# First layer of a two-layer selective-scan network: the sum over states kept in PSUM, powers taken downwards, carries of two states gathered on 128 rows

## The chip, the cores and the metric

The kernel runs on one core of a Trainium2 chip. The metric is the device time of the whole program in microseconds (us), the median of three runs. All arithmetic is fp32. The engines are PE (TensorE), DVE (VectorE), ACT (ScalarE), POOL (GpSimd) and SP (the queue that issues DMAs); each takes its own instructions in program order.

## The reference

The input is x, 4 images of 64x64 positions with 192 channels. Two layers follow, each a projection to 384 inner channels, four selective scans over the positions (rows, columns and both backwards), a norm, a gate and a projection back. The change touches the scans of the first layer alone. For each image, each of its four directions k and each inner channel d they are

```
delta = softplus(dts + bias)                      # per position l and channel d
h_n(l) = exp(-n * delta(l)) * h_n(l-1) + delta(l) * u(l) * B_n(l)     n = 1..16
y(l)   = sum over n of C_n(l) * h_n(l)  (+ u(l) * D)
```

because the logs of A are those of 1 to 16, so that state n decays with n times the same exponent (the kernel tests this, and falls back on another path where it does not hold).

## The kernel before

**Tiling.** The 4096 positions of a direction are cut into rounds of `RW` = 31 (`NR` = 133 rounds). A tile has 128 rows, two halves of 64. A half has two directions with 31 positions each, and 2 more rows, the last ones, in which a state enters from the round before and leaves for the next. The free dimension `W` = 1536 is four images of 384 channels. With cum, the sum of delta inside the round, each state is a matrix product: x_n = delta*u*exp(n*(cum-shift)) is multiplied by a masked triangle that carries B_n, and the product by C_n*exp(-n*(cum-shift)).

**A step** is one state of one round, so there are 16 steps in a round. Each step s has these parts:

- `grown` (L1005) makes x of step s+6 from x of the step before by one more factor g: 512 columns on DVE (its factor g0 lies in PSUM), 1024 on POOL. For the first state it starts from `dtu`.
- `decay` (L990, ACT) makes es = exp(-n*cum) over all 1536 columns, and `b_mask` (L996, ACT) four masked triangles `b`, two steps ahead.
- `mix` (L1011, PE) multiplies b by x into a bank q. It is called four times in a step, with two 64x64 matmuls each.
- `weigh` (L1021, DVE) makes t = q * C_n * es, four times in a step, from PSUM into SBUF.
- `add_y` (L1030, PE) sums t over the states, two steps later, by matmuls with the identity into four banks yp: again eight matmuls in a step.
- `carry_out` and `carry_in` (L985, L981, SP) take the last two rows of each half of t to DRAM, and bring them 16 steps later into the same two rows of x.

**A round's preparation** lies between the steps of the rounds before it. `Round.steps` gives it offsets, and `planned` places it. `v` (PE) and `parts` (ACT) make the argument of softplus; `exp`, `log` (ACT), `plus`, `rest`, `total` (POOL) take it apart; `delta` (PE) sums two terms of it by identity matmuls with the halves turned over; `keep_dt` (ACT) and then `times_u` (DVE, L878) read the result; `sums` (PE) and `grow` (ACT) make g; `sums_d` (PE) and `keep_sums` (ACT) make cum; `keep_total` stores its last rows to DRAM for a test of the range after the scans (`reach`, L668 and L670). `load_xd`, `load_u`, `load_bc`, `load_y` and `store_y` are DMAs on SP. `end_y` (DVE, L927) adds yp to the y of earlier rounds.

**What sets the order.** All five queues are written out by hand in one loop over s (`manual_schedule`): program order is the order of emission. The PSUM banks are four for yp, one for g0 and three, one pool, for q and for the bank `m` of the preparation. In one pass of the loop ACT gets decay and the masks of s+2 and then its planned work; DVE gets the four `weigh` of s, with planned work after the second, and then `grown`; PE gets the `mix` of s+1 and the `add_y` of s-2 in turn, with planned work after the second pair and at the end.

Of the kernel before, what the change touches and what calls it, by code (L numbers as in the profile page):

```python
# [15 lines left out]
L = HW * HW  # L16
# [13 lines left out]
RW = 31  # L30
# [542 lines left out]
class FirstLayer(Stage):  # L573
# [3 lines left out]
    def __init__(self, tc, ctx, consts, w, dram, good):  # L577
# [4 lines left out]
        self.uT, self.bc, self.xd, self.y_row, self.y_col, self.tot, self.carry, self.zeros = dram  # L582
# [10 lines left out]
        self.mask = load("mask", [128, HALF])  # L593
# [6 lines left out]
        self.shift = wp.tile([128, 1], F32, name="shift_f")  # L600
        nc.vector.memset(self.shift, -SHIFT)
# [5 lines left out]
        with tc.tile_pool(name="d4", bufs=1) as pd:  # L607
# [24 lines left out]
            nc.sync.dma_start(self.y_col[L // 2 - 2 : L // 2 + 2], z[:4].rearrange("p (b e) -> p b e", b=NB))  # L632
            for n in range(NS):
                nc.sync.dma_start(self.carry[n].rearrange("c q r f -> (c q) (r f)"), z[:KD])
# [28 lines left out]
    def reach(self):  # L663
        nc = self.tc.nc
        with self.tc.tile_pool(name="reach", bufs=1) as pool:
            n = NR * KD * W // 128
            t = pool.tile([128, n], F32, name="tot")
            nc.sync.dma_start(t, self.tot.rearrange("(p f) -> p f", p=128))  # L668
            top = pool.tile([128, 1], F32, name="tot_top")
            nc.vector.tensor_reduce(top, t, mybir.AxisListType.X, ALU.max)  # L670
            nc.vector.tensor_scalar(top, top, REACH / NS - SHIFT, None, ALU.is_le)
            nc.vector.tensor_tensor(self.good, self.good, top, ALU.min)
# [71 lines left out]
    def scans(self):  # L744
        nc, tc = self.tc.nc, self.tc
        with ExitStack() as ctx:
            pool = lambda name, bufs, **k: ctx.enter_context(tc.tile_pool(name=name, bufs=bufs, **k))
            p1, p2 = pool("b1", 1), pool("b2", 2)
            p_x, p_e, p_t, p_b = pool("bx", 7), pool("be", 4), pool("bt", 4), pool("bb", 3)
            ps_y = pool("psy", 1, space=bass.MemoryType.PSUM)  # L750
            ps_q = pool("psq", 3, space=bass.MemoryType.PSUM)
            ps_g = pool("psg", 1, space=bass.MemoryType.PSUM)
            ident, mask, tri = self.ident, self.mask, self.tri
            N = NR * NS
            sets = lambda t: t.rearrange("p (b e) -> p b e", b=NB)
# [3 lines left out]
            top = lambda k: k // 2 * HALF + k % 2 * RW  # L759

# [7 lines left out]
            c_in = [p1.tile([128, NB, NS], F32, name=f"c_in{i}") for i in range(2)]  # L768
            for b, c in zip(b_in, c_in):
                nc.sync.dma_start(b, self.w["b_last"])  # L770
                nc.vector.memset(c, 1.0)
# [6 lines left out]
            def runs(k, r, most, turned=False):  # L778

                row, lo, n = block(k, r)  # L780
                while n:
                    m = min(n, most, HW - lo % HW) if turned else min(n, most)
                    yield row, lo, m
                    row, lo, n = row + m, lo + m, n - m
# [6 lines left out]
            class Round:  # L791

                def __init__(self, r):
                    self.r = r
                    self.b, self.c = b_in[r % 2], c_in[r % 2]
# [9 lines left out]
                def load_u(self):  # L805
                    for k in range(KD):
                        for row, lo, n in runs(k, self.r, 16, k % 2 == 1):
# [3 lines left out]
                def load_bc(self):  # L811
                    for k in range(KD):
                        at = k * 2 * NS
                        for row, lo, n in runs(k, self.r, RW, k % 2 == 1):
# [3 lines left out]
                            for c in range(2):  # L818
                                to = c * HALF + k % 2 * RW + row
                                of = bc_dram[:, 2 * c : 2 * c + 2, at + NS : at + 2 * NS]  # L820
                                nc.sync.dma_start(
                                    self.c[to : to + n, k // 2 * 2 : k // 2 * 2 + 2], place(of, k, lo, n)
                                )

                def bank(self):
                    self.m = ps_q.tile([128, LC], F32, name="m", tag="q")
# [38 lines left out]
                def rest(self):  # L865
                    nc.gpsimd.tensor_tensor(self.d, self.e, self.d, ALU.subtract)  # L866

                def total(self):
                    nc.gpsimd.tensor_tensor(self.l, self.l, self.d, ALU.add)  # L869

                def delta(self, i):
                    one = lambda a, b: ident[half(a), half(a)]
                    self.swap(i, [(one, lambda a, b, t=t: t[half(a), cols(b)]) for t in (self.l, self.up)])
# [11 lines left out]
                def sums(self, i):  # L885
                    self.bank()
                    nc.tensor.matmul(self.m, tri, self.dt[:, wide(i)], start=True, stop=True)  # L887

                def grow(self, i):
                    if i == 0:  # L890
                        self.g0 = ps_g.tile([128, LC], F32, name="g0")
                        to = self.g0
                    else:
                        if i == 1:
                            self.g = p2.tile([128, W - LC], F32, name="g")
                        to = self.g[:, wide(i - 1)]
                    nc.scalar.activation(to, self.m, AF.Exp, bias=shift)  # L897
# [4 lines left out]
                def keep_sums(self, i):  # L902
                    if i == 0:
                        self.cum = p2.tile([128, W], F32, name="cum")
                    nc.scalar.activation(self.cum[:, cols(i)], self.m[:, :DI], AF.Identity, bias=shift)

                def keep_total(self):
                    to = tot[self.r * KD * W : (self.r + 1) * KD * W]
                    for c in range(2):
                        nc.sync.dma_start(to.rearrange("(c q f) -> c q f", c=2, q=2)[c], end(self.cum, c))  # L910

                def load_y(self):
                    r = self.r
                    if r == MIDDLE:
                        for k in (2, 3):
                            nc.sync.dma_start(yold[top(k) : top(k) + RW], zeros)
                    for k in range(KD):
                        if (k % 2 == 1 and r < MIDDLE) or (k > 1 and r == MIDDLE):
                            continue
                        for row, lo, n in runs(k, r, 16):  # L920
                            row += top(k)
                            nc.sync.dma_start(sets(yold)[row : row + n], (y_row, y_col)[k % 2][lo : lo + n])

                def end_y(self, b):
                    if b == 2:
                        self.y = p1.tile([128, W], F32, name="yt")
                    nc.vector.tensor_add(self.y[:, cols(b)], self.yp[b][:, :DI], yold[:, cols(b)])  # L927

                def store_y(self):
                    for k in range(KD):  # L930
                        for row, lo, n in runs(k, self.r, 16):
                            row += top(k)
                            to, of = (y_row, y_col)[k % 2][lo : lo + n], sets(self.y)[row : row + n]
# [5 lines left out]
                def steps(self):  # L939

                    s = lambda f, *a: (lambda: f(*a))
                    r = [(-32, "sp", self.load_xd), (-20, "sp", self.load_u), (-8, "sp", self.load_bc)]
                    for i in range(NB):
                        r += [(i - 24, "pe", s(self.v, i)), (i - 23, "act", s(self.parts, i))]
                        r += [(i - 14, "pe", s(self.delta, i)), (i - 13, "dve", s(self.times_u, i))]
                        r += [(i - 13, "act", s(self.keep_dt, i))]
                        r += [(i - 8, "pe", s(self.sums_d, i)), (i - 7, "act", s(self.keep_sums, i))]
                    r += [(-19, "act", self.exp), (-18, "act", self.log), (-18, "pool", self.plus)]
                    r += [(-17, "pool", self.rest), (-16, "pool", self.total)]
                    r += [(-10, "pe", s(self.sums, 1)), (-9, "act", s(self.grow, 1))]  # L950
                    r += [(-9, "pe", s(self.sums, 2)), (-8, "act", s(self.grow, 2))]
                    r += [(-7, "pe0", s(self.sums, 0)), (-7, "late", s(self.grow, 0))]
                    r += [(-3, "sp", self.keep_total), (6, "sp", self.load_y), (NS + LAG + 1, "sp", self.store_y)]
                    for i, b in enumerate((2, 0, 3, 1)):
                        r += [(NS + LAG, f"dve{i}", s(self.end_y, b))]
                    return r

            w_dt, one, shift, zeros, tot = self.w_dt, self.one, self.shift, self.zeros, self.tot
            uT, bc_dram, xd_dram, y_row, y_col, carry = self.uT, self.bc, self.xd, self.y_row, self.y_col, self.carry
            MIDDLE = L // 2 // RW  # L960
            LAG = 2
# [12 lines left out]
            xs, es, bs, qs, ts = {}, {}, {}, {}, {}  # L974
            of = lambda s: (rounds[s // NS], s % NS)
            end = lambda t, c: t[c * HALF + 2 * RW : (c + 1) * HALF]

            def carry_in(s):
                for r in range(2):
                    to = end(xs[s], r).rearrange("q (c f) -> q c f", c=2)  # L980
                    nc.sync.dma_start(to, carry[s % NS][:, :, r, :].rearrange("c q f -> q c f"))  # L981

            def carry_out(s):
                for c in range(2):
                    nc.sync.dma_start(carry[s % NS][c].rearrange("q r f -> q (r f)"), end(ts[s], c))  # L985

            def decay(s):
                it, n = of(s)
                es[s] = p_e.tile([128, W], F32, name="es")
                nc.scalar.activation(es[s], it.cum, AF.Exp, scale=-(n + 1.0))  # L990

            def b_mask(s, i):
                it, n = of(s)
                if s not in bs:
                    bs[s] = p_b.tile([128, NB, HALF], F32, name="b")
                nc.scalar.mul(bs[s][:, i, :], mask, it.b[:, i, n : n + 1])  # L996

            def grown(s, engine):
                it, n = of(s)
                if s not in xs:  # L1000
                    xs[s] = p_x.tile([128, W], F32, name="x")
                part = slice(0, LC) if engine is nc.vector else slice(LC, W)
                x = it.dtu if n == 0 else xs[s - 1]
                g = it.g0 if engine is nc.vector else it.g
                engine.tensor_tensor(xs[s][:, part], x[:, part], g, ALU.mult)  # L1005

            def mix(s, r, j):
# [775 lines left out]
```

## Time and profile before

| what | us |
|---|---|
| median of three runs | 11298.84 (11295.07 to 11307.86) |
| profiled execution | 11290.43, span 11288.6 |
| first `weigh` to last `weigh` | 712.8 to 9533.7 |
| PE, DVE, ACT, POOL busy, share of the span | 87%, 70%, 71%, 60% |
| the same in one round, 5000 to 5066.5 | 60.0, 49.4, 49.9, 47.6 of 66.5 |

The scans of the first layer take 8821 of the 11289 us; the projection before them takes some 0.7 ms and what follows them 1.75 ms. A group line reads: line, engine, operation, output<-inputs, shape, count | busy time, mean ns of one | idle time of the engine ahead of it, and who ended most of it. A timeline line reads: start, length, engine, line, operation, count, and the idle time ahead of it with its releaser. PE shows each fp32 matmul as two instructions, so a `mix` call has four.

### The profile page before, as it was taken

What the parts mean: (1) busy time and instruction counts of PE and PEld (TensorE: products, weight loads), DVE (VectorE), ACT (ScalarE), POOL (GpSimd) and SP (SyncE); (2) the same over time, 40 slices, a digit from 0 to 9 for tenths busy, and PEclk for the clock granted to TensorE, in tenths of its full rate; (3) what the DMA queues carried; (4) which work ended last, traced back from release to release, by engine and by line L of the source; (5) the groups of instructions that cost most, each with busy time, mean ns of one, the idle gap of its engine ahead of it and who ended that gap; (6) DMA issues with size and microseconds to landing.
All of it is one profiled execution on the core that took longest, in us unless ns stands there. A gap on an engine that the chain in (4) does not pass through costs nothing. (4 is left out here: it accounts for less than half of the span.)

```text
span 11288.6 us, 244138 instructions
## 1 busy us (share of the span) xinstructions
PE 9828.6 (87%) x85544; PEld 4313.8 (38%) x85544; DVE 7946.4 (70%) x13822; ACT 7976.7 (71%) x15454; POOL 6738.5 (60%) x2912
## 2 busy tenths in 40 slices
PE   8989899989998999898989998899889997488677
PEld 4533333333333333333333333333333333454366
DVE  2347777777777777777777777777777777478675
ACT  3357777777777777777777777777777776566587
POOL 0047777777777777777777777777777775300270
PEclk9999999999999999999999999999999999788688
DMA  4421111111111111112222222222222223943358
GB/s 148 165 83 42 45 43 45 42 45 43 45 42 45 43 45 42 45 43 47 50 49 51 48 50 49 51 48 50 49 51 48 50 48 87 265 137 120 143 143 276
DMA packets 667786, 836.25 MB, mean 74 GB/s; under 512 B 305814, under 2 KB 558243, under 8 KB 665822
## 3 DMA queue, kind: packets, MB, share of 16 engines
q1 hardware_dynamic: 661566, 813.80, 27.3%
q0 software_dynamic: 4992, 6.68, 0.4%
q8 instruction: 698, 11.44, 0.4%
q14 instruction: 530, 4.34, 0.1%
HBM read 468.75 MB, written 351.35 MB: 73 GB/s over the span
## 5 line engine op out<-in xcount | busy, mean ns | idle before, releaser
L1011 PE MATMUL q<-x,b 64*64 64x384 f32 x34048 | 6151.7, 492 | 858.4 <-DVE dtu L878 618.9
L1005 POOL TENSOR_TENSOR x<-x,g 128x1024 f32<-128x1024 f32 x1995 | 4730.0, 2371 | 2299.3 <-PE q L1011 1668.3
L1030 PE MATMUL yp<-t,ident 64*64 64x384 f32 x34048 | 6097.5, 494 | 0.0
L1021 DVE SCALAR_TENSOR_TENSOR t<-q,c_in,es 128x384 f32<-128x384 f32 x8512 | 4945.1, 614 | 1082.5 <-PE q L1011 505.9
L1011 PEld LDWEIGHTS q<-x,b 64*64 64x64 f32 x34048 | 2172.8, 132 | 3836.0 <-DVE t L1021 1451.1
L990 ACT ACTIVATE es<-cum 128x1536 f32<-128x1536 f32 x2128 | 3152.5, 1481 | 0.9 <-DVE t L1021 0.9
L1030 PEld LDWEIGHTS yp<-t,ident 64*64 64x64 f32 x34048 | 2069.6, 132 | 757.4 <-issue 660.6
L996 ACT ACTIVATE b<-mask_f,b_in 128x64 f32<-128x64 f32 x8512 | 2255.6, 341 | 3.5 <-PE yp L1030 3.1
L1005 DVE TENSOR_TENSOR x<-x,g 128x512 f32<-128x512 f32 x1995 | 1353.9, 679 | 0.2
L883 ACT COPY dt<-m 128x384 f32<-128x384 f32 x532 | 255.2, 480 | 1359.8 <-PE m L833 1359.8
L878 DVE TENSOR_TENSOR dtu<-m,ut 128x384 f32<-128x384 f32 x532 | 296.8, 558 | 1221.8 <-ACT dt L883 1221.8
L460 PE MATMUL pp<-xT,w_in 96*128 96x512 f32 x1536 | 710.4, 614 | 20.5 <-ACT pad L1230 20.0
L897 ACT ACTIVATE g<-m,shift_f 128x512 f32<-128x512 f32 x399 | 271.2, 680 | 634.2 <-PE m L887 634.1
L862 POOL TENSOR_SCALAR d<-e 128x1536 f32<-128x1536 f32 x133 | 196.5, 1477 | 676.6 <-ACT e L854 676.6
L1244 DVE SCALAR_TENSOR_TENSOR acc<-pad,conv_w_s,acc 128x2048 f32<-128x2048 f32 x192 | 440.7, 2345 | 47.8 <-ACT acc L1242 46.5
L833 PE MATMUL m<-w_dtk_f,xd 26*64 26x384 f32 x2128 | 460.0, 511 | 8.9 <-DMA xd<-xd 8.9
L866 POOL TENSOR_TENSOR d<-e,d 128x1536 f32<-128x1536 f32 x133 | 464.2, 3490 | 0.1
L869 POOL TENSOR_TENSOR l<-l,d 128x1536 f32<-128x1536 f32 x133 | 463.1, 3482 | 0.1
L887 PE MATMUL m<-dt,steps_f 128*128 128x512 f32 x798 | 450.1, 646 | 0.0
L833 PE MATMUL m<-l,ident 64*64 64x384 f32 x2128 | 433.9, 486 | 15.5 <-POOL l L869 15.5
L833 PE MATMUL m<-up,ident 64*64 64x384 f32 x2128 | 433.6, 486 | 0.0
L1005 POOL TENSOR_TENSOR x<-dtu,g 128x1024 f32<-128x1024 f32 x133 | 313.8, 2359 | 200.2 <-PE q L1011 163.4
(201 smaller groups left out, 8258.1 us busy)
## 6 DMA issues: line engine op xcount, KB each, us to landing
x<-carry SPq DMA_DIRECT2D x4256, 12.0 KB
carry<-t SPq DMA_DIRECT2D x4256, 12.0 KB
ut<-uT SPq DMA_DIRECT2D x528, 96.0 KB
zg<-gate SPq DMA_DIRECT2D x64, 768.0 KB
ut<-uT SPq DMA_DIRECT2D x414, 90.0 KB
yold<-y_row SPq DMA_DIRECT2D x263, 96.0 KB
y_row<-yt SPq DMA_DIRECT2D x263, 96.0 KB
y_col<-yt SPq DMA_DIRECT2D x263, 96.0 KB
```

What stands on the lines that cost most here:

```text
L460: self.tc.nc.tensor.matmul(pp, self.w_in[:, i, e * 128 : (e + 1) * 128], self.xT[:, i, t * LC : (t + 1) * LC], start=(i == 0), stop=(i == ...
L833: nc.tensor.matmul(self.m[half(b), :DI], w(a, 2 * b + j), t(a, 2 * b + j), start=n == 0, stop=n == len(terms) - 1, skip_group_check=True,)
L866: nc.gpsimd.tensor_tensor(self.d, self.e, self.d, ALU.subtract)
L869: nc.gpsimd.tensor_tensor(self.l, self.l, self.d, ALU.add)
L887: nc.tensor.matmul(self.m, tri, self.dt[:, wide(i)], start=True, stop=True)
L990: nc.scalar.activation(es[s], it.cum, AF.Exp, scale=-(n + 1.0))
L996: nc.scalar.mul(bs[s][:, i, :], mask, it.b[:, i, n : n + 1])
L1005: engine.tensor_tensor(xs[s][:, part], x[:, part], g, ALU.mult)
L1011: nc.tensor.matmul(q[half(c), :DI], bs[s][half(r), b, :], xs[s][half(r), cols(b)], start=True, stop=True, skip_group_check=True,)
L1021: nc.vector.scalar_tensor_tensor(ts[s][:, cols(i)], qs.pop((s, r, j))[:, :DI], it.c[:, i, n : n + 1], es[s][:, cols(i)], ALU.mult, ALU.mult)
L1030: nc.tensor.matmul(it.yp[2 * c + j][half(r), :DI], ident[half(c), half(c)], ts[s][half(c), cols(2 * r + j)], start=n == 0, stop=n == NS - ...
L1244: nc.vector.scalar_tensor_tensor(acc, part(tap), weight(tap), acc, ALU.mult, ALU.add)
```

## The change

The sum over n is evaluated as a polynomial from the highest power down. Four accumulators `accs` stay in PSUM for the whole stage. In each step `mix` adds the product of state n onto them, and `weigh` multiplies them in place by the ratio C_n/C_(n-1) and by fd = exp(shift-cum), so that the next, lower state is added to it. The states thus go from 16 to 1 (`state(s)` = 16 - s%16): x starts at exp(16*(cum-shift)) and is multiplied by f = exp(shift-cum) from step to step.

- Removed: `decay` over 1536 columns, `add_y`, the tile t, `rest` and `total` on POOL, and the DRAM copy of the totals with its reading back in `reach`.
- Rows: `RW` is 30 and NR 137. Each half now has four rows at its end: the carry of an even state goes through one pair, that of an odd state through the other. `masks` has a form for each, `hold` holds a finished even carry while the odd state is added.
- Carries: at every second step (odd state) `keep_end` copies all four accumulators to SBUF on ACT, ahead of `weigh`; `shrink` (two DMAs) spreads the four last rows of each half over 64 rows of 96; `decay` (ACT, now 128x96), `settle` (POOL) and one `carry_out` DMA follow.
- Preparation: `delta` has four terms in place of two (it does the work of `rest` and `total`); `fall` makes f and `first` the first power g, both on ACT from the same bank; `keep_sums` writes fd as well as cum; `invert` (DVE) and `ratios` (POOL) make the ratios. The first x of a round is made by POOL alone, in three pieces. `m` has three banks of its own.
- End of a round: `add_old` adds the old y by a matmul onto each accumulator, `end_y` copies it out on ACT; both stand in the loop ahead of the `mix` that starts the accumulator anew.
- `load_y`, `store_y`, `load_u` cut their DMAs elsewhere; `test` (DVE) keeps a running maximum of the totals.

```diff
-RW = 31
+RW = 30
...
-                def rest(self):
-                    nc.gpsimd.tensor_tensor(self.d, self.e, self.d, ALU.subtract)
-                def total(self):
-                    nc.gpsimd.tensor_tensor(self.l, self.l, self.d, ALU.add)
                 def delta(self, i):
-                    one = lambda a, b: ident[half(a), half(a)]
-                    self.swap(i, [(one, lambda a, b, t=t: t[half(a), cols(b)]) for t in (self.l, self.up)])
+                    terms = [(ident, self.e), (minus, self.d), (ident, self.l), (ident, self.up)]
...
+                def add_old(self, i):
+                    for c in c_tiles:
+                        nc.tensor.matmul(
+                            accs[i][half(c), :DI], ident[half(c), half(c)], yold[half(c), cols(i)],
+                            start=False, stop=True, skip_group_check=True,
+                        )
...
-                    nc.vector.tensor_add(self.y[:, cols(b)], self.yp[b][:, :DI], yold[:, cols(b)])
+                    nc.scalar.copy(self.y[:, cols(i)], accs[i][:, :DI])
...
+                        r += [(i - 16, "pe", s(self.delta, i)), (i - 15, "dve", s(self.times_u, i))]
+                        r += [(i - 15, "act", s(self.keep_dt, i))]
+                        r += [(i - 9, "pe", s(self.sums_d, i)), (i - 8, "act", s(self.keep_sums, i))]
                     r += [(-19, "act", self.exp), (-18, "act", self.log), (-18, "pool", self.plus)]
+                    for i in (1, 2):
+                        r += [(i - 12, "pe0", s(self.sums, i)), (i - 11, "act", s(self.fall, i)), (i - 11, "act", s(self.first, i))]
+                    r += [(-7, "pe0", s(self.sums, 0)), (-6, "act", s(self.first, 0)), (-6, "act", s(self.fall, 0))]
...
+            def keep_end(s, i):
+                if i == 0:
+                    sxs[s] = p2.tile([128, W], F32, name="sx")
+                nc.scalar.copy(sxs[s][:, cols(i)], accs[i][:, :DI])
...
+                        accs[i][half(c), :DI], bs[s][half(r), b, :], xs[s][half(r), cols(b)],
+                        start=s % NS == 0, stop=state(s) == 1, skip_group_check=True,
...
+                part = accs[i][:, :DI]
                 nc.vector.scalar_tensor_tensor(
-                    ts[s][:, cols(i)], qs.pop((s, r, j))[:, :DI], it.c[:, i, n : n + 1], es[s][:, cols(i)], ALU.mult, ALU.mult
+                    part, part, it.ratio[:, i, n - 1 : n], it.fd[:, cols(i)], ALU.mult, ALU.mult
                 )
...
+                    if pair(s - 1):
+                        shrink(s - 1)
+                    if pair(s - 5):
+                        carry_out(s - 5)
                     if on(s + AHEAD - 2):
                         carry_in(s + AHEAD - 2)
                     planned(s, "sp")
+                    if pair(s):
+                        for i in order:
+                            keep_end(s, i)
+                    if pair(s - 2):
+                        decay(s - 2)
                     if on(s + 2):
-                        decay(s + 2)
                         for i in range(NB):
                             b_mask(s + 2, i)
                     planned(s, "act")
...
+                    for at, i in enumerate(order):
                         if on(s):
+                            weigh(s, i)
+                        if at == 1:
                             planned(s, "dve")
                     if on(s + AHEAD):
                         grown(s + AHEAD, nc.vector)
+                    for at, i in enumerate(order):
+                        if on(s) and state(s) == 1:
+                            of(s).add_old(i)
+                            of(s).end_y(i)
                         if on(s + 1):
+                            mix(s + 1, i)
+                        if at == 1:
                             planned(s, "pe0")
                     planned(s, "pe")
```

## The prediction

> **What bounds the kernel now.** I read the page first, its busy times and groups:
>
> ```profile
> PE 9828.6 (87%) x85544; PEld 4313.8 (38%) x85544; DVE 7946.4 (70%) x13822; ACT 7976.7 (71%) x15454; POOL 6738.5 (60%) x2912
> ...
> L1030 PE MATMUL yp<-t,ident 64*64 64x384 f32 x34048 | 6097.5, 494 | 0.0
> L1021 DVE SCALAR_TENSOR_TENSOR t<-q,c_in,es 128x384 f32<-128x384 f32 x8512 | 4945.1, 614 | 1082.5 <-PE q L1011 505.9
> ...
> L990 ACT ACTIVATE es<-cum 128x1536 f32<-128x1536 f32 x2128 | 3152.5, 1481 | 0.9 <-DVE t L1021 0.9
> ```
>
> PE looks full, but the change takes half of its matmuls away, so its share says little about the time after. Then DVE's timeline over one round, for the steps one by one:
>
> ```profile
> 5036.41 2.20 DVE L1021 SCALAR_TENSOR_TENSOR t<-q,c_in,es 128x384 f32<-128x384 f32 x4
> 5038.52 0.68 DVE L1005 TENSOR_TENSOR x<-x,g 128x512 f32<-128x512 f32 x1
> 5039.11 2.20 DVE L1021 SCALAR_TENSOR_TENSOR t<-q,c_in,es 128x384 f32<-128x384 f32 x4
> ...
> 5046.37 1.14 DVE L1021 SCALAR_TENSOR_TENSOR t<-q,c_in,es 128x384 f32<-128x384 f32 x2
> 5049.77 0.56 DVE L878 TENSOR_TENSOR dtu<-m,ut 128x384 f32<-128x384 f32 x1 [2.25 <-ACT dt L883]
> 5050.24 1.13 DVE L1021 SCALAR_TENSOR_TENSOR t<-q,c_in,es 128x384 f32<-128x384 f32 x2
> 5051.30 0.68 DVE L1005 TENSOR_TENSOR x<-x,g 128x512 f32<-128x512 f32 x1
> 5051.89 1.14 DVE L1021 SCALAR_TENSOR_TENSOR t<-q,c_in,es 128x384 f32<-128x384 f32 x2
> ```
>
> The reader is to see two kinds of step. A bare one takes 5039.11-5036.41 = 2.70 us: DVE without a gap. One with `times_u` takes 5051.89-5046.37 = 5.52. The other steps with planned work took 3.0 to 6.2. A round took 66.5 us, of which DVE worked 49.4 and ACT 49.9: **no engine is full; in-order queues waiting for one another set the time.** So the question is what the new queues wait for. PE's timeline ahead of that `times_u`, then ACT's:
>
> ```profile
> 5047.04 0.54 PE L1011 MATMUL q<-x,b 64*64 64x384 f32 x2 [0.71 <-DVE t L1021]
> 5047.06 0.54 PE L1030 MATMUL yp<-t,ident 64*64 64x384 f32 x2
> 5047.42 0.49 PE L1011 MATMUL q<-x,b 64*64 64x384 f32 x2
> 5047.43 0.49 PE L1030 MATMUL yp<-t,ident 64*64 64x384 f32 x2
> 5047.75 0.81 PE L833 MATMUL m<-l,ident 64*64 64x384 f32 x4
> 5048.40 0.81 PE L833 MATMUL m<-up,ident 64*64 64x384 f32 x4
> ```
>
> ```profile
> 5022.93 0.49 ACT L850 ACTIVATE e<-m 128x384 f32<-128x384 f32 x1 [0.21 <-PE m L833]
> 5023.31 0.49 ACT L851 ACTIVATE up<-m 128x384 f32<-128x384 f32 x1
> ...
> 5049.26 0.48 ACT L883 COPY dt<-m 128x384 f32<-128x384 f32 x1 [2.11 <-PE m L833]
> ```
>
> The prices, all from this round: a `weigh` lasts 0.61, the next starts 0.53 later, `grown` on DVE takes 0.59 of the queue; from the start of a `weigh` to the matmul that waits for it 0.67; a pair of matmuls 0.87 (5047.04 to 5047.91), its row half free again after 0.71; each identity term of `delta` 0.65, two terms 1.46; PE's end to ACT or DVE 0.05 to 0.08. A small ACT copy lasts 0.48 and takes 0.38 of the queue (5022.93 to 5023.31), with a bias 0.58 and 0.49, at 512 columns with a bias 0.59; four masks take 0.95; `exp` and `log` 1.37 and 1.47.
>
> [...] `times_u` and `keep_dt` only read m, and DVE waits 2.25 us for ACT. [...] No row here has DVE writing PSUM[...]. ACT's g took 0.66 into PSUM (5015.05) and 0.69 into SBUF (5004.64), so I take 0.53. [...] after 2.71 us of idle at 725.8, two terms of `delta` took 2.8, at a clock of 0.51.
>
> **The change part by part, by queue and round** (16 steps).
>
> PE loses 128 of its `mix`/`add_y` matmuls in 256, and gains 16 for `delta` and 8 for `add_old`. It was not waited for by its amount, so this is worth nothing by itself: `add_y` had no idle time of its own. But each accumulator is now a chain: `weigh`, `mix`, (`keep_end`,) `weigh`. From one `weigh` to the next on the same bank that is 0.67+0.87+0.07 = 1.6, with the copy 2.1; DVE comes back after 2.71. So a bare step stays at 2.71.
>
> DVE: 64 `weigh` as before, one `grown` and four additions of `end_y` fewer (0.59+1.9), plus `invert` and `test` (some 0.2 each, near the 0.15 to 0.3 us of its small instructions). ACT loses 16 `es` (1.38 each, 22) and gains 32 copies (12.2), 8 small `decay` (0.25 each, an estimate from the 64-column mask's 0.24), 3 `first`, 4 exponentials in `keep_sums`, 4 `end_y`: +20 us. POOL loses 6.97 (`rest`, `total`), gains 1.2 for the third piece of the first x, 0.35 for each of 8 `settle` (estimate from 2.37 at 1024 and 3.49 at 1536 columns) and `ratios`: 45 us, still ahead by six steps, which is also what hides a late `settle` with the `grown` behind it. SP: per two states four `carry_out` become two `shrink` and one spread store, at 0.27 to 0.7 each; the carries have three steps, some 12 us, before `settle`, and seven more before they are read. All other cut DMAs lie as far ahead as before. I cost these at nothing; with that cover gone, POOL's next x is late first.
>
> The steps where queues wait, walked through in program order (s%16):
>
> - **1 to 4, `times_u`.** `delta` starts when the last `mix` is out, about when DVE's step begins; four terms 0.16+4*0.65 = 2.76, copy 0.5, then `times_u`, two `weigh`, `grown`. In 1 and 2 this comes to 5.15; in 3 and 4 it starts behind that `mix` on its own row half, 5.65. Sum 21.6 (before: 4*5.5 = 22).
> - **5 to 8.** DVE's pace, 4*2.71; `sums` between the `mix` calls adds 0.2 and 0.5; at 9 ACT is 0.7 late. Sum 12.3.
> - **9 and 10.** `keep_end` stands in ACT's queue behind all that was planned, and `weigh` behind it. From `keep_end`(9) to (11): copies 1.52, `decay` 0.25, masks 2*0.95, `keep_sums` 2*0.98, `parts` 2*0.77, `first` and `fall` 1.18: 8.35. DVE alone needs 4.8.
> - **11 to 14.** The same count: 4.47+1.72, then, with `exp` and `log`, 4.09+2.42: 12.7. DVE alone 10.8.
> - **15 and 16, the end.** ACT reaches `end_y` at 2.2 after DVE's step 15 begins. Then PE may not issue `add_old` of the next bank before `mix` of this one, which waits for this `end_y`: per bank 0.48+0.05+0.71+0.86+0.05 = 2.15, three times. Last `mix` 1.4 later, `weigh` 0.53, `grown` 0.59: 11.2. DVE alone 5.4.
>
> The sum is **66.15 us a round, against 66.5**: 4.13 a step. But there are 137 rounds. Before, 8821/66.5 = 132.65 rounds fit between first and last `weigh`; now 136.65*66.15 = 9039, +218. After the scans, the load of totals and its reduction held up the y loads from about 9546 to 9562: -15. The profiled execution goes from 11290 to 11493; the median stood 8 above it: **11501 us**.
>
> **Rivals.**
>
> *ScalarE keeps ahead, faster.* Place: steps 9 to 14. If its 40-odd instructions there overlap more, DVE sets the pace: 21.05 falls to 15.6, the round to 60.7, the scans to 8295, the whole to 10757. For it: ACT's groups in the round sum to 53.9 us, its busy time is 49.9. Against it: my prices are queue paces, which have that overlap in them. It decides below 64.65 a round, 1.5 less than mine: 0.04 us on each.
>
> *Writing PSUM is dear, slower still.* [...]
>
> *PE goes cold.* Gaps of 2 us (steps 10 and 14) might halve its clock: `delta` +2.6 four times, the end +4: 14 a round, 13400. Against it: in dtu steps PE sat idle 1.2 us and the clock read 1.00.
>
> *The chain overlaps at the end of a round*, so nothing is lost there: 5.8 less, 10700. Against it, the order of emission.
>
> *It doesn't do what it says*: a fallback taken would add milliseconds; nothing in the data changes the tests.
>
> **How the numbers follow.** Mine 0.56 (its own range, 65 to 67.5 a round, 11345 to 11690), dear PSUM or missed waits 0.12, cold PE 0.02, ScalarE ahead 0.22 and overlap 0.08, most of these two only in part. 0.2% is 23 us, what a measurement of this kernel tells from nothing. Slower 0.67, same 0.05, faster 0.28. A fifth left out: 62.6 to 69.5 a round, 11020 to 11960.
>
> **What would show it.** Bare steps of 2.7 and `times_u` steps of 5.1 to 5.7; `weigh` waiting for `keep_end` (ACT) at 9 to 15; `mix` waiting for `end_y` about 2.1 apart; ACT without idle time from 9 to 15; PEclk 1.0. Rounds under 64.6 would make it wrong, and so would DVE mostly waiting for DMA or POOL.

## The result and the profile after

The changed kernel takes **12945.69 us** (12937.09 to 12955.09, four runs) against 11302.89 for the kernel before on the same chip: ratio 1.1454 (1.1434 to 1.1474). The forecast was 11501, at most 11960; "slower" was right, the size was not. The profiled execution has a span of 12953.2 us. Its scans last from 694.7 to 11174.3, which is 76.7 us a round (forecast 66.15, before 66.5); all that lies outside them takes 2474 us, 6 more than before.

From the page after: busy times, the clock in 40 slices, and the two large groups of a step.

```profile
PE 11100.9 (86%) x59376; PEld 4382.1 (34%) x59376; DVE 7981.2 (62%) x13766; ACT 7775.3 (60%) x20653; POOL 6596.0 (51%) x4362
...
PEclk9987778777777877878777778777777777778778
...
L1069 PE MATMUL acc<-x,b 64*64 64x384 f32 x35072 | 6396.5, 616 | 1066.9 <-DVE acc L1077 606.4
...
L1077 DVE SCALAR_TENSOR_TENSOR acc<-acc,ratio,fd 128x384 f32<-128x384 f32 x8768 | 4988.2, 617 | 2174.3 <-PE acc L1069 942.3
```

The same clock row in the page before:

```profile
PEclk9999999999999999999999999999999999788688
```

The reader is to see that PE has 30% fewer instructions (59376 against 85544) and yet is busy 1272 us longer, and that the granted clock has fallen from 9 to 7 and 8 all through the scans (mean over the span 0.965 before, 0.794 after). DVE's `weigh` costs what it did, 617 ns against 614. So no new work on these two engines fills the time: PE does less work at a lower clock.

The granted clock has two levels in these traces, 1.0 and 0.5, and changes on a grid of 3.413 us: all its 767 changes in the kernel after and all 107 in the kernel before lie within 0.03 us of it. The table of windows, cut at those periods, shows what goes with it; its counts take in every instruction that touches a window. Columns: window, length, busy time (instructions) of PE, weight loads, DVE, ACT and POOL, granted clock, DMA. After:

```profile
5035.09:5038.51 3.42, 3.12 (x28) 1.27 (x24) 3.42 (x7) 3.42 (x10) 2.50 (x2) 1.00 0.39 92
5038.51:5041.92 3.41, 1.47 (x10) 0.20 (x4) 2.18 (x4) 3.41 (x10) 3.33 (x3) 1.00 0.03 9
5041.92:5045.33 3.41, 2.63 (x8) 0.79 (x8) 3.09 (x5) 0.68 (x3) 3.38 (x3) 0.50 0.15 31
...
5058.99:5062.40 3.41, 3.21 (x15) 0.88 (x12) 0.93 (x2) 1.44 (x5) 0.57 (x1) 0.50 0.12 20
5062.40:5065.82 3.42, 3.20 (x14) 1.40 (x16) 2.33 (x5) 0.00 (x0) 0.98 (x1) 0.50 0.11 27
```

And before, in the thinnest place of its round, the `times_u` steps that the prediction looked at:

```profile
5046.35:5049.76 3.41, 2.17 (x16) 0.75 (x16) 1.17 (x3) 1.30 (x6) 3.33 (x3) 1.00 0.00 0
```

In the window 5038.51 to 5041.92 PE runs 10 instructions, not none, and the next windows are at half clock. There its busy time says nothing: 3.2 of 3.41 us for 14 or 15 instructions. Now all windows of the scans, with the instructions that begin in each. Before, 2565 windows were at full clock and followed by another at full clock; 2562 of them had 16 or more matmul instructions and the least had 14; the clock dropped twice, after 12. After, it dropped 325 times, 279 of these behind a window with at most 14 (over a third of all behind one with at most 8), and 1003 windows at half clock were followed by another, with a median of 11. **The kernel before stood just above the edge in its `times_u` steps (16 in a window), and the change, which halves the large matmuls, fell below it.** Once down it mostly stays down (1003 windows at half clock followed by another, 325 drops). My reading, which no run isolates, is that slow matmuls stretch the step, and that a stretched step has fewer of them in a window.

What half clock does to the two chains that the prediction had priced: ACT's `end_y` at the end of a round, and two of the four terms of `delta` on PE (line 855):

```profile
5042.13 0.48 ACT L965 COPY yt<-acc 128x384 f32<-128x384 f32 x1
5045.54 0.48 ACT L965 COPY yt<-acc 128x384 f32<-128x384 f32 x1 [2.94 <-PE acc L957]
```

```profile
5063.95 1.49 PE L855 MATMUL m<-e,ident 64*64 64x384 f32 x4
5065.23 1.49 PE L855 MATMUL m<-d,minus_f 64*64 64x384 f32 x4
```

The links are 3.4 us apart (priced 2.15) and a term takes 1.28 (priced 0.65).

### The profile page after: what moved, and what is told of

The parts are those of the page before. It is cut to its first block, busy times and chain, and to the rows that moved or that the text cites. A ratio compares the mean times of both kernels' runs of the same rounds, so it can differ in the third digit from the quotient of the medians.

```text
span 12953.2 us, 206811 instructions
## 1 busy us (share of the span) xinstructions
PE 11100.9 (86%) x59376; PEld 4382.1 (34%) x59376; DVE 7981.2 (62%) x13766; ACT 7775.3 (60%) x20653; POOL 6596.0 (51%) x4362
## 5 line engine op out<-in xcount | busy, mean ns | idle before, releaser
L1069 PE MATMUL acc<-x,b 64*64 64x384 f32 x35072 | 6396.5, 616 | 1066.9 <-DVE acc L1077 606.4
L1063 POOL TENSOR_TENSOR x<-x,f 128x1024 f32<-128x1024 f32 x2055 | 4848.5, 2359 | 3659.6 <-DMA y_row<-yt 1018.0
L1077 DVE SCALAR_TENSOR_TENSOR acc<-acc,ratio,fd 128x384 f32<-128x384 f32 x8768 | 4988.2, 617 | 2174.3 <-PE acc L1069 942.3
L1069 PEld LDWEIGHTS acc<-x,b 64*64 64x64 f32 x35072 | 1983.4, 157 | 4990.8 <-DVE acc L1077 2956.5
L1029 ACT COPY sx<-acc 128x384 f32<-128x384 f32 x4384 | 1919.0, 515 | 1013.1 <-PE acc L1069 674.9
L1050 ACT ACTIVATE b<-masks_f,b_in 128x64 f32<-128x64 f32 x8768 | 2381.2, 378 | 0.0
L957 PE MATMUL acc<-yold,ident 64*64 64x384 f32 x2192 | 1238.7, 760 | 194.6 <-DVE acc L1077 194.6
L1063 DVE TENSOR_TENSOR x<-x,f 128x512 f32<-128x512 f32 x2055 | 1388.3, 676 | 8.0 <-POOL x L1059 7.9
L855 PE MATMUL m<-d,minus_f 64*64 64x384 f32 x2192 | 571.1, 604 | 1.6 <-POOL d L885 1.6
L855 PE MATMUL m<-e,ident 64*64 64x384 f32 x2192 | 551.2, 582 | 2.6 <-ACT e L876 2.6
```

What stands on the lines that cost most here:

```text
L855: nc.tensor.matmul(self.m[half(b), :DI], w(a, 2 * b + j), t(a, 2 * b + j), start=n == 0, stop=n == len(terms) - 1, skip_group_check=True,)
L957: nc.tensor.matmul(accs[i][half(c), :DI], ident[half(c), half(c)], yold[half(c), cols(i)], start=False, stop=True, skip_group_check=True,)
L1029: nc.scalar.copy(sxs[s][:, cols(i)], accs[i][:, :DI])
L1050: nc.scalar.mul(bs[s][:, i, :], masks[:, n % 2, :], of(s).b[:, i, n - 1 : n])
L1063: engine.tensor_tensor(xs[s][:, part], xs[s - 1][:, part], f, ALU.mult)
L1069: nc.tensor.matmul(accs[i][half(c), :DI], bs[s][half(r), b, :], xs[s][half(r), cols(b)], start=s % NS == 0, stop=state(s) == 1, skip_group ...
```

## The experiments

Two theories stand against each other. **A**: the queues are as predicted, and the clock of PE makes the difference. **B**: the new waits in the queues are themselves longer than priced, and a low clock is only their by-product. All ratios are to the kernel before, run beside; "cold" is time at half clock in a round, in us, and a step without any is warm; a "link" is the stretch from one `end_y` to the next at the end of a round. A label in brackets is the name of a run, by which the expectations speak of one another. Step lengths run from the first `weigh` of a step to that of the next.

A fit over the 136 rounds of the kernel after gives round = 63.1 + 0.406 * cold, r = 0.98, with a mean of 33.4 us cold: 13.6 us a round. It is a correlation, and its 63.1 lies outside the rounds that it is fitted to (none has less than 16 us cold); the runs below change one side of it.

**More matmuls without a reader** (e8). The changed kernel, with nothing moved:

```
+def busy(n):
+    spare = ps_m.tile([128, LC], F32, name="m")
+    nc.tensor.matmul(spare[:, :n], ident, fill[:, :n], start=True, stop=True, skip_group_check=True)
...
     of(s).end_y(i)
+    busy(256)
...
     planned(s, "pe0")
+    if on(s) and s % NS in (1, 2, 3, 4):
+        busy(256)
...
     planned(s, "pe")
+    if on(s) and s % NS in (12, 13, 14):
+        busy(LC)
```

> The changed kernel with nothing moved; PE gets matmuls that nobody reads (64 columns fewer than a step of work would need): 256 columns into a spare tile of the m buffers after the second mix of steps 1 to 4, at each of the four end_y links, and 512 columns at the ends of steps 12, 13 and 14. A (the clock of PE falls to half where few matmuls are issued, queues else as predicted): clock above 0.95, times_u steps 5.15 and 5.67, last step of the round 7 to 8.5, a round 63 to 66 us, the whole 11090 to 11500. B (the queues themselves wait longer, the clock is a by-product): added matmuls only add, 12900 or more.

Measured: **11520.72 us**, ratio 1.0188 (1.017 to 1.0206), clock 0.948, 3.0 us cold and **66.28 us a round**. A's account holds, though each of its figures but the `times_u` steps is missed by a little: the clock is 0.948 for 0.95, a round 0.3 and the whole 21 us above the upper end, the last step of the round 6.4 rather than 7 to 8.5. B's fails by 1400 us. Work was added to PE, and the kernel became 1425 us faster; a round is 10.4 us shorter. Through the scans the page's clock row reads 9 as before the change. ACT's links and the same terms of `delta`:

```profile
5012.70 0.47 ACT L965 COPY yt<-acc 128x384 f32<-128x384 f32 x1
5014.80 0.48 ACT L965 COPY yt<-acc 128x384 f32<-128x384 f32 x1 [1.62 <-PE acc L957]
```

```profile
5032.03 0.81 PE L855 MATMUL m<-e,ident 64*64 64x384 f32 x4
5032.68 0.81 PE L855 MATMUL m<-d,minus_f 64*64 64x384 f32 x4
```

The links are 2.1 apart with the added matmul inside each, hidden behind the wait for `end_y`; a term takes 0.65. This kernel is the prediction's, group of steps by group of steps (table below).

**Two earlier tries at the same** (e2 and e6). The first moved f0 to SBUF to have a bank for the unread result; the second left f0 in PSUM and took the bank from `m`. Both added 256 columns at each step's end and at each link, 512 at the ends of steps 10, 12 and 14.

```
-self.f0 = ps_f.tile([128, LC], F32, name="f0")      # first
+self.f0 = p2.tile([128, LC], F32, name="f0")
-ps_m = pool("psm", 3, space=bass.MemoryType.PSUM)   # second
+ps_m = pool("psm", 2, space=bass.MemoryType.PSUM)
+ps_s = pool("pss", 1, space=bass.MemoryType.PSUM)
```

> The control plus matmuls whose result nobody reads, into the freed bank: one of 256 columns at the end of each step and ahead of each mix that waits for end_y, 512 columns at the ends of steps 10, 12 and 14. They only add work. Theory A (PE's clock falls to one half in stretches with few matmuls; the queues are as predicted): clock above 0.95, rounds of 63 to 66 us in place of 76.7, 11090 to 11500 us. Theory B (the waits in the queues are themselves longer than predicted, a low clock only goes along with them): no faster than the control, 12900 us or more, and slower by up to half a us a step (1000 us).

> The unread matmuls of e2 again, but f0 stays in PSUM and the free bank comes from m, which keeps two banks in place of three. In e1 and e2 DVE's grown with f0 in SBUF took 1.4 us in place of 0.68, so they were no clean test. A: the unread matmuls keep the clock above 0.95, 63 to 66 us a round, 11090 to 11500 us, if two banks for m cost nothing; up to 11700 if they do. B: 12500 us or more.

Measured: 12033.73, ratio 1.0651 (1.0633 to 1.0668), clock 0.963; and 12295.93, ratio 1.0887 (1.0868 to 1.0905), clock 0.935. Both are faster than B allowed (12900 and 12500), and both missed A's whole by hundreds of us. The `times_u` steps 2 to 4 were A's (5.15 and 5.67 in both), but the bank was not free: with two banks for `m` step 10 took 7.4 us rather than 5.4, and PE was cold in steps 10 and 11 of 112 of 136 rounds; what the first paid is in the next run. So by themselves they did not decide; the run above did.

**f0 in SBUF alone** (e1), to know what the first of these paid.

> The control of the next run: the changed kernel with f0 in SBUF in place of PSUM, nothing else, which frees one PSUM bank. DVE's grown read 512 columns from PSUM in 0.68 us, and nothing waits for it alone. Both theories: within 0.5% of the changed kernel, 12880 to 13010 us, mean clock 0.79.

Measured: 12609.86, ratio 1.1175 (1.1155 to 1.1194), clock 0.848: *faster* than the kernel after, against all accounts. DVE's group of `grown`:

```profile
L1062 DVE TENSOR_TENSOR x<-x,f 128x512 f32<-128x512 f32 x2055 | 2889.3, 1406 | 8.0 <-POOL x L1058 7.9
```

It went from 676 to 1406 ns with both inputs in SBUF, and the bare step 9 from 2.7 to 3.3. The kernel was faster all the same since only 22.3 us of a round were cold, against 33.4. Why the slower DVE left PE warmer was not isolated. The trace shows a `grown` of DVE beside a multiplication of POOL:

```profile
5003.39 2.36 POOL L1062 TENSOR_TENSOR x<-x,f 128x1024 f32<-128x1024 f32 x1 [4.42 <-DMA y_row<-yt]
5003.90 2.40 DVE L1062 TENSOR_TENSOR x<-x,f 128x512 f32<-128x512 f32 x1
```

The DVE instruction ends 0.55 us after POOL's. So do all 1237 that began while a multiplication of POOL ran, to within 0.08 us; the 541 of 2055 that met no POOL instruction took 0.68 us, as with f0 in PSUM.

**Shorter chains in place of more matmuls.** All four `add_old` ahead of the first `mix` (first, e3), or `rest` and `total` back on POOL and two terms in `delta` (second, e4), or both (third, e5).

```
+if on(s) and state(s) == 1:
+    for i in order:
+        of(s).add_old(i)
 for at, i in enumerate(order):
     if on(s) and state(s) == 1:
-        of(s).add_old(i)
         of(s).end_y(i)
...
-terms = [(ident, self.e), (minus, self.d), (ident, self.l), (ident, self.up)]
+terms = [(ident, self.l), (ident, self.up)]
...
+r += [(-17, "pool", self.rest), (-16, "pool", self.total)]
```

> The changed kernel with the four add_old of a round issued together, ahead of the first mix of the next round, in place of each behind the end_y and mix before it. Queues alone, at full clock, give 4 to 5 us less a round (11.2 to 6.6), at half clock 6 to 7: B says 12000 to 12400. A says more: the longest stretch with few matmuls is gone, so that PE is cold in fewer rounds: 11200 to 12000, clock above 0.85.

> One part of the change undone: rest and total are back on POOL and delta has two terms. B: 1.3 us less at each of four steps, if POOL's two extra operations of 3.5 us are in time, 700 us at most: 12200 to 12900. A: the part is worth 1.3 us where PE is warm and 2.6 where it is cold, but the cold stretch at the end of a round stays: 11700 to 12500, clock 0.8 to 0.87.

> The two edits of e3 and e4 together: add_old ahead, and delta with two terms. Alone they took 1086 and 883 us off. B (each shortens its own waits, the clock is a by-product): at most their sum, 10980 us or more. A (both also bring the matmuls closer together, and a cold stretch ends when they are close enough): more than the sum, since the steps that stayed cold in e3 were those of delta; at full clock the medians of the single steps of e3 and e4 give 57 us a round, so 10100 to 10700 us, clock above 0.93.

Measured: 11859.89, ratio 1.0506 (1.0483 to 1.053), clock 0.863, 18.6 cold; 12062.62, ratio 1.0684 (1.0666 to 1.0702), clock 0.819; 12071.72, ratio 1.0695 (1.0677 to 1.0713), clock 0.816, 26.8 cold. The first two lie in A's ranges and below B's. The first takes step 0, the end of the round, from 10.9 to 2.7 us (step 15 grows from 4.6 to 5.9), and the clock, which no longer drops there, keeps `times_u` steps 1 and 2 at 5.15. The second brings `times_u` steps to 3.9-4.6 where they are warm, and leaves step 0 cold at 10.7. The third lies far above A's range and within B's bound: it should have had both gains and was no faster than the second. PE's timeline shows the new wait ahead of `delta`:

```profile
5008.53 1.50 PE L855 MATMUL m<-l,ident 64*64 64x384 f32 x4 [3.39 <-POOL l L891]
```

POOL's `rest` and `total`, 3.4 us each, are not done when the shortened round asks for them: step 1 took 9.3 us, PE stood idle and went cold in it and in the steps behind it.

The first of the three shows something more. PE's windows at the end of a round, where the four `add_old` now stand:

```profile
6540.09:6543.51 3.42, 1.69 (x10) 0.47 (x8) 2.64 (x3) 3.42 (x12) 3.34 (x3) 1.00 0.06 17
6543.51:6546.92 3.41, 2.25 (x21) 1.38 (x24) 2.22 (x4) 1.50 (x5) 3.13 (x3) 1.00 0.14 30
```

Only eight instructions begin in the first window, all of `add_old`, and the clock holds. It held in this way behind 164 windows with 8 to 14 instructions, 158 of them with `add_old` in them, and dropped behind 140 others with at most 14. So the edge of 14 to 16 instructions, read from the two kernels above, is not a rule for every kind of matmul.

**One step later**: the third of these with `delta`, `times_u` and `keep_dt` moved one step later, without (e9) and with (e10) unread matmuls (256 columns in steps 2 to 4 and at the links, 512 at the ends of steps 12 to 14).

```
-r += [(i - 16, "pe", s(self.delta, i)), (i - 15, "dve", s(self.times_u, i))]
-r += [(i - 15, "act", s(self.keep_dt, i))]
+r += [(i - 15, "pe", s(self.delta, i)), (i - 14, "dve", s(self.times_u, i))]
+r += [(i - 14, "act", s(self.keep_dt, i))]
```

> The changed kernel with the four add_old ahead of the first mix of their step, delta of two terms with rest and total on POOL, and delta, times_u and keep_dt one step later, so that POOL's two subtractions are done in time. A: if the shorter chains keep the clock at full, a round of 58 to 62 us, 10400 to 11000; if PE, with still fewer matmuls, falls to half clock in the times_u steps, clock 0.80 to 0.88 and 66 to 69 us, 11500 to 11950. B (the queues are what is long, whatever the clock): with the links and POOL's lateness gone, below 11000 even at a clock of 0.85 or less.

> The kernel of the run before with unread matmuls added: 256 columns after the second mix of steps 2 to 4 and at the links, 512 at the ends of steps 12 to 14. A: clock above 0.95, a round of 58 to 61 us, 10400 to 10900, faster than the kernel before. B: no faster than the run before, by the added PE time 0 to 3 us a round slower.

Measured: **11128.95**, ratio 0.984 (0.9823 to 0.9856), 12.9 us cold, 63.7 a round; and **11115.85**, ratio 0.9833 (0.9816 to 0.9849), 3.7 cold, 63.2 a round. Both are 14% below the changed kernel and 1.6 to 1.7% below the kernel before. The first lies between A's two cases and above B's bound, and tells them apart no further. In the second the `times_u` steps fell to 3.9-4.6, but it missed A's range by 216 us, and as a whole it was no faster than the first, as B had it: its step 0 took 5.4 in place of 2.7 (the added matmuls now stand between the `mix` calls with no wait to hide them) and step 15 took 6.6 in place of 5.95, which gave back what 9 us less of cold time had saved.

**add_old ahead with the unread matmuls** (e11), a miss:

> The changed kernel with the four add_old ahead of the first mix, and the unread matmuls of the first of these four runs. A: clock above 0.95, the last step of the round near 3, a round of 61.5 to 64 us, 10900 to 11250. B: no better than with add_old ahead alone (11860), or slower.

Measured: 11764.32, ratio 1.0402 (1.0385 to 1.0419), clock 0.931, 68.1 a round. Less than 100 us better than without, and worse than the unread matmuls alone. Step 0 went back from 2.7 to 5.4 for the reason just given, and step 12 was cold in some 120 of 136 rounds (4.6 us, not 3). Neither B nor A had that.

**The last step, and a cheaper test** (e12). `test` is DVE's maximum of two SBUF tiles in the middle of the last step. The run starts from the one step later with unread matmuls, but has none of these at the links, and its 512 columns stand at the ends of steps 9 to 12.

```
-nc.vector.tensor_tensor(far, far, self.tot, ALU.max)
+nc.vector.tensor_reduce(far[:, self.r : self.r + 1], self.tot, mybir.AxisListType.X, ALU.max)
```

> The kernel with add_old ahead, two terms of delta one step later, unread matmuls after the second mix of steps 2 to 4 and at the ends of steps 9 to 12 but none at the links; and test, the running maximum of the totals on DVE, is no longer an addition of two SBUF tiles (1.87 us each, half-way through the last step) but a reduction of one tile into a column of its own. A with a DVE instruction that waits for POOL when both its inputs are in SBUF: test falls to 0.3 us or less, the last step of the round from 6.1 to 4.5 or less, step 12 near 3; a round of 57.5 to 61 us, 10350 to 10800, clock above 0.95. Rival for test (a slow form whatever its inputs): 1.5 us or more still, the last step still near 6, 10800 to 11000. B: nothing gained on the two kernels before it, 11100.

Measured: 11201.39, ratio 0.9912 (0.9899 to 0.9926), 8.7 us cold, 64.0 a round. `test`'s group in the kernel after, and then in this one:

```profile
L937 DVE TENSOR_TENSOR far_f<-far_f,tot 128x96 f32<-128x96 f32 x137 | 255.9, 1868 | 3.7 <-DMA tot<-cum 3.7
```

```profile
L943 DVE TENSOR_REDUCE far_f<-tot 128x1 f32<-128x96 f32 x137 | 33.3, 243 | 3.8 <-DMA tot<-cum 3.8
```

The instruction fell from 1.87 to 0.24 us, the last step from 5.95 (in the kernel one step later without unread matmuls) to 4.36; step 0 is 2.7 again without matmuls at the links, and step 12 was never cold. The run alone doesn't put the rival for `test` out, a form slow whatever its inputs, since the form changed along with the inputs. The traces do: in the kernel after, every one of the 137 `test` ran beside a multiplication of POOL and ended 0.11 to 0.12 us after it, and a `grown` with two SBUF inputs that met none took 0.68 us (above). The reduction of one input took at most 0.25 us beside the same multiplications. Yet the round did not shrink, and A's range was missed by 400 us. POOL's timeline, and PE's wait behind it:

```profile
4536.10 3.45 POOL L888 TENSOR_TENSOR d<-e,d 128x1536 f32<-128x1536 f32 x1
4539.50 2.37 POOL L1070 TENSOR_TENSOR x<-x,f 128x1024 f32<-128x1024 f32 x1
4541.82 3.44 POOL L891 TENSOR_TENSOR l<-l,d 128x1536 f32<-128x1536 f32 x1
```

```profile
4545.31 0.86 PE L855 MATMUL m<-l,ident 64*64 64x384 f32 x4 [2.06 <-POOL l L891]
```

The time gained at the round's end is given back in the step of the first `delta` (median 8.0 us, 5.3 with `test` slow): it waits for POOL's `total`, and the clock drops there in 94 of 136 rounds. POOL without a gap from `rest` on is what is late next.

**The kernel before, made thinner** (e7). `keep_dt` three times in place of once makes its `times_u` steps longer with the same matmuls in them.

```
-nc.scalar.copy(self.dt[:, cols(i)], self.m[:, :DI])
+for _ in range(3):
+    nc.scalar.copy(self.dt[:, cols(i)], self.m[:, :DI])
```

> The kernel before, with keep_dt's copy of 0.38 us made three times in place of once, so that each of the four steps with times_u gets 0.76 us longer and PE does nothing in that time. In those steps the kernel before had 15 to 16 matmul instructions in a window of 3.4 us, the fewest that it had anywhere in the scans with a full clock. B: 133 rounds of four steps, 0.76 us each, 404 us: 11700. A: such windows fall below what keeps the clock up, PE runs cold in those steps, and they get several us longer: 12100 to 13500, mean clock 0.85 or less.

Measured: 12041.69, ratio 1.066 (1.0642 to 1.0678), clock 0.942, 72.1 us a round, between the two accounts. The four steps took 6.5 to 7.6 us rather than 5.5. The fit gives round = 70.2 + 0.427 * cold with 4.5 us cold, so by this fit some 1.9 of the added 5.6 us are clock and the rest is the copies. The clock dropped 157 times rather than twice, each time behind a window with at most 12 matmul instructions (106 other windows of 12 kept the clock). So the old kernel can be pushed over the same edge, by one more us in a step.

## Why the prediction was wrong

The table sets the prediction's sums (us a round) beside the means of 136 rounds.

| steps | predicted | after | with unread matmuls |
|---|---|---|---|
| 1 to 4, `times_u` | 21.6 | 25.7 | 21.5 |
| 5 to 8 | 12.3 | 13.8 | 12.1 |
| 9 and 10 | 8.35 | 8.35 | 8.35 |
| 11 to 14 | 12.7 | 13.5 | 13.3 |
| 15 and 16 (index 15 and 0 of the next round) | 11.2 | 15.4 | 11.0 |
| a round | 66.15 | 76.7 | 66.3 |

- **The step that failed** is "PE loses 128 of its `mix`/`add_y` matmuls … so this is worth nothing by itself", and with it the chance of 0.02 for the rival "PE goes cold". Those matmuls held the clock: without them it fell to 0.794, at a cost of 10.4 us a round. The rival's price was near: 14 a round and 13400 against 10.55 above my sum and 12945.69; the end of the round cost 4.2 more (I said 4), the `times_u` steps 4.1 and the steps behind them 1.5 (I said 10.4 together).
- **Why I put it aside.** I wrote "in dtu steps PE sat idle 1.2 us and the clock read 1.00" and took idle time as what counts; that it does was an assumption of mine, which no trace had shown. The one drop that I cited for it, at 725.8, was not behind an idle window: the clock fell at 725.07, before the 2.71 us of idle time had ended, behind a window in which 12 matmul instructions had begun. Nor were most of those in the kernel after, where the window ahead of a drop had a median of 14. Read by count, the kernel before would have shown me 12 as too few, and 16 in its `times_u` steps: little to take away.
- **Right at full clock**: bare steps 2.7, `times_u` steps 5.15 and 5.67, `weigh` behind `keep_end` in steps 9 to 14, links of 2.1. That 66.28 comes so near 66.15 is in part luck: the 77 rounds of that run without cold time took 65.5, 0.6 under the sum. Writing PSUM in place is not dear (`weigh` took 617 ns, against 614 from PSUM into SBUF; the size of that rival was an estimate that no trace had shown), ScalarE did not keep ahead in 9 and 10 (8.35 as priced), and the chain at the end did not overlap: these three rivals are out.
- **Mis-sized.** `test` 0.2, measured 1.87; `invert` 0.2, measured 0.54. In the kernel as changed `test` lies under ACT's way to `end_y`, so the sum of steps 15 and 16 held; with `add_old` ahead it came out and cost 1.6. Steps 11 to 14 exceed their price by 0.6 in the kernel with unread matmuls because step 12 was still cold in 58 rounds there; in the 77 rounds without cold time they take 12.4. Outside the scans I said -15 and it was +6.
- **The rounds.** 137 rounds in place of 133 cost what was said: 136.65*66.28 = 9057 in the kernel with unread matmuls, and the whole is 11520.72 against a forecast of 11501.

That A holds for the kernel after is shown by that run. Its forecasts of the size were met in two runs (e3, e4), narrowly missed in the run with unread matmuls, and missed in the rest, in part through waits that nobody had priced.

Which quantity the clock follows is only bounded. Take the columns of each matmul instruction, weighted by the size of its tile as a share of 128x128, the largest tile here. Then the kernel after drops below some 1440 such columns in 3.41 us (15 of the 64x64 instructions of 384) and returns from half clock at about 1600; 4 to 5% of its windows fall on the wrong side, no fewer than by a plain count at the drop. With unread matmuls, whose tiles are 128x128, the weighting is better than the count (29 windows wrong against 57, of 2533). Over the full-clock windows of all fourteen kernels (31575, with 2394 drops) it leaves 5.2% wrong, most of them windows with `add_old` that kept the clock; with each instruction of `add_old` counted twice, 2.4%. Why it should count twice is not shown.

## What to carry to other kernels

Before taking matmuls away from a kernel whose PE is "not the bound", count the matmul instructions in each clock period of its thinnest stretch, and compare with the least count that has kept the full clock there; a busy share cannot show this, since a slowed PE looks full (here 3.0 of 3.41 us busy with 11 instructions, medians at half clock). Compare like with like: matmuls of another shape, and even `add_old` of the same shape, counted differently here, so the number 16 is not to be carried over, and the granted clock of the new kernel decides. If the new count is lower, shorten the chains there, or keep a few unread matmuls in places where PE waits anyway (where it doesn't wait they cost their own time, as in step 0 of the run one step later). And when a wait is taken out of a chain, look at which queue arrives next: here POOL's, in two of the experiments.

## What the runs showed of the hardware that was not expected

- The clock fell with PE at work: in the kernel after, 279 of 325 drops stood behind windows in which at most 14 matmul instructions began (median 14, mostly 64x64 by 384 columns); in the kernel before, full clock held in 2562 windows of 16 or more.
- The count is not the quantity: with `add_old` ahead, full clock held behind 164 windows of 8 to 14 instructions, and a rule by weighted columns fits all fourteen kernels better when `add_old` counts twice (2.4% of windows wrong against 5.2%).
- Half clock lasted: in the kernel after, 1003 windows at half clock were followed by another, with a median of 11 instructions while PE showed as busy for 3.0 us of 3.41 (median).
- Adding matmuls that nobody reads made the kernel 11% faster (12945.69 to 11520.72).
- A DVE operation on 96 columns took 1.87 us with two SBUF inputs beside POOL's multiplications, always ending 0.11 to 0.12 us after one of them, and 0.24 as a reduction of one input. On 512 columns it took 0.68 us when POOL was still, and ended 0.55 us after POOL's multiplication when it began during one.
